# Frequency attention with real circulant matrices kept on chip, two rows a step

## The chip, the cores and the metric

The kernel runs on one core of a Trainium2 chip. The metric is the time on the device in microseconds (us), the median of several executions. All data are 32-bit floats.

## The reference

Two layers work on `x` of shape (8, 128, 128, 128): 8 images, 128 channels, 128 x 128 pixels. The change lies in the first layer, after a group norm:

```python
xf = jnp.fft.fft2(x)                                   # per image and channel
qf = xf.reshape(b, HEADS, hd, h * w)                   # 8 heads of 16 channels
qn = _l2norm_lastdim(qf)
attn_f = jnp.einsum('bhcn,bhdn->bhcd', qn, qn) * temp_f[None]
attn_f = jax.lax.complex(softmax(attn_f.real, axis=-1), softmax(attn_f.imag, axis=-1))
out_cplx = jnp.einsum('bhcd,bhdn->bhcn', attn_f, qf)
out_f = jnp.abs(jnp.fft.ifft2(out_cplx)).reshape(b, c, h, w)
...                                                    # gate in frequency: out_f_l
fsa = _conv(jnp.concatenate([out_f, out_f_l], axis=1), projf_w)
...                                                    # spatial attention: out_s, out_s_l
ssa = _conv(jnp.concatenate([out_s, out_s_l], axis=1), projs_w)
return fsa + ssa                                       # the layer adds x
```

The second layer is a selective scan over the pixels. It follows another group norm and is not touched.

## The kernel before

The kernel is one program of five stages, written with a tile framework that gives each engine a list of instructions and adds the waits.

Stage A normalises the images into `XN` (and a mirrored copy `XR`), and makes the 1x1 convolutions for the spatial attention (`PQKVX`). There POOL copies pieces of `x` into planes (L318) while DVE scales `x` (L334). Stage B makes the frequency attention matrix of each image, `aF`, and the gated frequency output `OFL`. Stage C makes the spatial attention, and writes its values `VS` and the local part `LS`. Stage D, which the change rewrites, makes the frequency output `out_f` and the projection of all four parts. Stage E is the second layer; there every instruction is recorded under L157, the line of the helper `InOrder`, which issues the instructions of an engine in the written order.

Stage D takes the images one after the other. For each it has two phases.

In the first phase the attention works along the image's rows instead of on a transform. `aF[:, b]` holds 128 cosine sums and 128 sine sums of the attention. `mix(i)` takes four rows of `XN` (`d_xn`, RB = 4) and the four rows' constants (`ker`, three 128 x 128 matrices a row, loaded from memory anew for every image). For each row one matmul with `aF` gives 256 columns (`d_a`, L641), and one DVE copy for two rows brings them to SBUF (`pq`, L642). `back(i)` runs one step later. For each row two accumulating matmuls of 256 columns with `ker` give the real and the imaginary part (`d_b`, L653 and L654). ACT squares both (`sq`, L655), POOL adds the squares (L656), and ACT writes the root into `of` (L657), which holds the whole image.

In the second phase the image is projected in 32 places of 512 pixels. Each place loads `OFL` (`d_of`) and `x` (`d_x`), every fourth place a band of `VS` and `LS` (`d_vs`, `d_ls`, 1 MB each). Four matmuls (L689 to L692) accumulate in `d_p`. DVE adds `d_x` and writes `x1` (L695), takes the statistics of the next group norm (L696), and POOL's queue stores it into `X1` (L697; the profile calls the tile `x` and the store `X`).

All loads of stage D stand in SP's queue. Pools with 3 buffers (`d_k`, `d_w`) or 2 (`d_v`) let loads run ahead; `of` has a single buffer. A load that waits for its buffer holds up the loads behind it in the queue.

Of the kernel before, what the change touches and what calls it, by code (L numbers as in the profile page):

```python
# [39 lines left out]
_CONSTS = [  # L40
    "ident", "group4", "mask", "neg", "c16", "s16", "first", "tc", "cm", "sm", "sneg", "a1", "a2", "blocks", "small",
    "cmp", "smp",
]


def _constants():
    i = np.arange(128)
    ang = 2 * np.pi * np.outer(i, i) / 128
    cos, sin = np.cos(ang), np.sin(ang)
    block = (i[:, None] // HD == i[None, :] // HD).astype(np.float64)  # L50
    u = np.arange(1, 64)

    tc = np.concatenate([cos[:, 64:65], sin[:, u], cos[:, u], cos[:, 0:1]], 1)
    a1 = np.concatenate([cos[64:65], 2 * sin[u], 2 * cos[u], cos[0:1]], 0) / HW
    a2 = np.concatenate([cos[64:65], 2 * cos[u], -2 * sin[u], cos[0:1]], 0) / HW
    made = {
        "ident": np.eye(128),
        "group4": (i[:, None] // 4 == i[None, :] // 4) / 4.0,
        "mask": block,
        "neg": (block - 1) * 1e30,  # L60

        "c16": block * np.cos(2 * np.pi * np.outer(i, i) / HD) / HD,
        "s16": block * np.sin(2 * np.pi * np.outer(i, i) / HD) / HD,
        "first": block * (i[None, :] % HD == 0) / HD,

        "cmp": cos.reshape(128, 32, 4).transpose(0, 2, 1).reshape(128, 128),
        "smp": sin.reshape(128, 32, 4).transpose(0, 2, 1).reshape(128, 128),
        "tc": tc, "cm": cos, "sm": sin, "sneg": -sin, "a1": a1, "a2": a2,
    }


    kind, quarter = i // 16 % 2, i // 32
    made["blocks"] = (kind[:, None] == i[None, :] // 64) & (quarter[:, None] == i[None, :] // 16 % 4)
    small = np.zeros((128, 128))
    small[:, 0:32] = i[:, None] % 32 == i[None, :32]
    small[:, 32:64] = kind[:, None] == i[None, :32] // 16
    small[:, 64:80] = i[:, None] % 16 == i[None, :16]
    small[:, 80:82] = kind[:, None] == i[None, :2]
    made["small"] = small

    ker = np.exp(2j * np.pi * np.outer(np.arange(HW), i) / HW).mean(1)
    ker = ker[(128 * (i[None, None, :] - i[:, None, None]) + i[None, :, None]) % HW]
    ker = np.stack([-ker.imag, ker.real, ker.imag], 2)
    return (
        np.concatenate([made[n] for n in _CONSTS], 1).astype(np.float32),
        ker.astype(np.float32),
    )
# [6 lines left out]
def _layout(a):  # L94
# [3 lines left out]
    o["consts"], o["ker"] = _constants()  # L98
# [4 lines left out]
    ws = [a[p + n + "1_w"].reshape(C, C) for n in "qkv"] + [f[:, :C], f[:, C:], s[:, rows], s[:, C:]]  # L103
# [64 lines left out]
def tile_kernel(ctx: ExitStack, tc: tile.TileContext, I: dict, out: bass.AP):  # L168
# [26 lines left out]
    def const(name, n=1):  # L195
        i = _CONSTS.index(name)
        return cst[:, i * 128 : (i + n) * 128]

    eye = const("ident")
# [14 lines left out]
    aF = keep.tile([128, B, 256], F32, name="aF")  # L214
# [144 lines left out]
    with tc.tile_pool(name="b_x", bufs=1) as xp_, tc.tile_pool(name="b_g", bufs=1) as gp_, tc.tile_pool(  # L359
        name="b_w", bufs=3  # L360
    ) as wk, tc.tile_pool(name="b_s", bufs=2) as sp_, tc.tile_pool(name="b_ps", bufs=8, space=PSUM) as psum:
        xh = xp_.tile([128, C, W], F32, name="xh")
# [16 lines left out]
        for b in range(B):  # L379
# [54 lines left out]
            nc.tensor.matmul(fp[:, :256], lhsT=att, rhs=const("c16", 2), start=True, stop=True)  # L434
            nc.vector.tensor_copy(aF[:, b, 0:128], fp[:, 0:128])
            nc.vector.tensor_tensor(aF[:, b, 128:256], fp[:, 128:256], const("first"), ALU.add)
# [172 lines left out]

    with tc.tile_pool(name="d_o", bufs=1) as op_, tc.tile_pool(name="d_v", bufs=2) as vp_, tc.tile_pool(  # L610
        name="d_k", bufs=3
# [3 lines left out]
        RB = 4  # L615
        of = op_.tile([128, W, RB, H // RB], F32, name="of")
        for b in range(B):
            ab = sp_.tile([128, 128], F32, name="ab")
            nc.vector.tensor_tensor(
# [5 lines left out]
            nc.tensor.matmul(mp[:, :128], lhsT=ab, rhs=weight("ps1"), start=True, stop=True)  # L625
            mT = sp_.tile([128, 128], F32, name="mT")
            nc.vector.tensor_copy(mT, mp[:, :128])
            st = sp_.tile([128, 32, 6], F32, name="st")
            live = {}

            def mix(i):

                xn = kp.tile([128, RB, W], F32, name="d_xn")
                nc.sync.dma_start(xn.rearrange("p h w -> p (h w)"), XN[b, :, i * RB * W : (i + 1) * RB * W])
                ker = kp.tile([128, RB, 3, 128], F32, name="ker")
                nc.sync.dma_start(ker, I["ker"][:, i * RB : (i + 1) * RB])
                pq = wk.tile([128, RB, 256], F32, name="pq")
                for j in range(0, RB, 2):
                    ps = psum.tile([128, 2, 256], F32, name="d_a", tag="ps")
                    for r in range(2):  # L640
                        nc.tensor.matmul(ps[:, r, :], lhsT=xn[:, j + r, :], rhs=aF[:, b, :], start=True, stop=True)  # L641
                    nc.vector.tensor_copy(pq[:, j : j + 2, :], ps)  # L642
                live[i] = (pq, ker)

            def back(i):

                pq, ker = live.pop(i)
                sq = wk.tile([128, RB, 2, 128], F32, name="sq")
                for j in range(0, RB, 2):
                    ps = psum.tile([128, 2, 256], F32, name="d_b", tag="ps")  # L650
                    for r in range(2):
                        kr = ker[:, j + r].rearrange("p t m -> p (t m)")
                        nc.tensor.matmul(ps[:, r, :], lhsT=pq[:, j + r, 0:128], rhs=kr[:, 128:384], start=True, stop=False)  # L653
                        nc.tensor.matmul(ps[:, r, :], lhsT=pq[:, j + r, 128:256], rhs=kr[:, 0:256], start=False, stop=True)  # L654
                    nc.scalar.activation(sq[:, j : j + 2], ps.rearrange("p r (t m) -> p r t m", t=2), AF.Square)  # L655
                nc.gpsimd.tensor_tensor(sq[:, :, 0, :], sq[:, :, 0, :], sq[:, :, 1, :], ALU.add)  # L656
                nc.scalar.activation(  # L657
                    of[:, :, :, i].rearrange("p m e -> p e m"), sq[:, :, 0, :], AF.Sqrt
                )

            n = H // RB
            for i in range(n + 1):
                if i < n:
                    mix(i)
                if i:
                    back(i - 1)
            off = of.rearrange("p m e j -> p (m e j)")
            band = {}
            for i in range(HW // 512):
                px = slice(i * 512, (i + 1) * 512)  # L670
                ld = {}
                for name, frm in (("of", OFL), ("x", I["x"])):
                    ld[name] = wk.tile([128, 512], F32, name=f"d_{name}")
                    nc.sync.dma_start(ld[name], frm[b, :, px])
                if i % 4 == 0:
                    for name, frm in (("vs", VS), ("ls", LS)):
                        band[name] = vp_.tile([128, 16, 4, 32], F32, name=f"d_{name}")

                        of_ = frm[b].rearrange("g (s k n) m -> s k g n m", s=4, k=2)[i // 8]
                        for kd in range(2):  # L680
                            nc.sync.dma_start(
                                band[name][64 * kd : 64 * kd + 64].rearrange("p n i j -> p n (i j)"),
                                of_[kd][:, :, i // 4 % 2 * 128 : i // 4 % 2 * 128 + 128],
                            )
                for name in ("vs", "ls"):
                    ld[name] = band[name][:, :, i % 4, :]
                ps = psum.tile([128, 512], F32, name="d_p", tag="ps")
                by4 = ps.rearrange("p (n j) -> p n j", j=32)
                nc.tensor.matmul(ps, lhsT=weight("pf2"), rhs=ld["of"], start=True, stop=False)  # L689
                nc.tensor.matmul(by4, lhsT=mT, rhs=ld["vs"], start=False, stop=False)  # L690
                nc.tensor.matmul(by4, lhsT=weight("ps2"), rhs=ld["ls"], start=False, stop=False)
                nc.tensor.matmul(ps, lhsT=weight("pf1"), rhs=off[:, px], start=False, stop=True)  # L692
                x1 = wk.tile([128, 512], F32, name="x1")
                nat = [t.rearrange("p (y j e) -> p y e j", y=4, e=4) for t in (x1, ld["x"])]
                nc.vector.tensor_tensor(nat[0], ps.rearrange("p (y e j) -> p y e j", y=4, e=4), nat[1], ALU.add)  # L695
                nc.vector.bn_stats(st[:, i, :], x1)  # L696
                nc.gpsimd.dma_start(X1[b, :, px], x1)  # L697
# [396 lines left out]
```

## Time and profile before

| | us |
|---|---|
| median of 3 executions | 21334.16 (21333.18 to 21354.21) |
| profiled execution, its own time | 21360.55 |
| profiled execution, span | 21358.5 |

| engine | busy us | share of the span | instructions |
|---|---|---|---|
| PE (matmul) | 18573.9 | 87% | 360816 |
| DVE | 13875.6 | 65% | 14884 |
| ACT | 11748.4 | 55% | 25436 |
| POOL | 11924.1 | 56% | 7116 |

The granted TensorE clock is 0.945 of full speed in the mean. Stage A ends at about 1850 us, B at 4300, C at 6520, D at 9120, and E takes the rest. A group of instructions in the profile is named by its line, its engine, its operation and its tiles (output<-inputs); after the bar stand the busy time, the mean time of one in ns, and the time that the engine was idle just before them with what ended it. Where a matmul works on 32-bit floats, the profile has two records for one matmul of the program.

### The profile page before, as it was taken

The page shows a single profiled execution, that of the slowest core. Times are in us where ns is not written, and L with a number is a line of the kernel's source. Part 1 is how long each engine was busy: PE and PEld are TensorE (multiplying, and loading weights), DVE is VectorE, ACT ScalarE, POOL GpSimd, SP SyncE. Part 2 cuts the span into 40 slices and gives each one's busy share as a digit, 9 for nine tenths or more (in the row PEclk, how much of TensorE's full clock was granted, in tenths as well). Part 3 has the DMA queues.
Part 4 walks back from the last instruction along what each step waited for, and adds up shares of the span by engine and source line. Part 5 has one row for each costly group of instructions (what it writes and reads, how often), then busy time and mean ns, then how long its engine had stood idle before and what let it go on. Part 6 is the DMA issues. An engine that isn't in the chain of part 4 may idle for free.

```text
span 21358.5 us, 802425 instructions
## 1 busy us (share of the span) xinstructions
PE 18573.9 (87%) x360816; PEld 10741.9 (50%) x360816; DVE 13875.6 (65%) x14884; ACT 11748.4 (55%) x25436; POOL 11924.1 (56%) x7116
## 2 busy tenths in 40 slices
PE   5647889889998898988989999898998989989898
PEld 3335667644546565644444444444444444444444
DVE  3332111133332333379999999999999999999999
ACT  2222222222222221267777777777777777777777
POOL 2221000000001111178889889898888888989888
PEclk8878999988889999999999999999999999999999
DMA  9996333255557888854444444444444444444443
GB/s 275 277 278 171 82 82 77 67 201 195 194 193 218 235 228 237 226 109 97 94 102 96 99 97 95 103 96 100 95 95 101 96 100 96 98 101 96 103 96 84
DMA packets 2989828, 2929.13 MB, mean 137 GB/s; under 512 B 1480494, under 2 KB 2275630, under 8 KB 2981667
## 3 DMA queue, kind: packets, MB, share of 16 engines
q1 hardware_dynamic: 2274818, 2537.53, 46.9%
q10 hardware_dynamic: 672672, 206.02, 4.5%
q0 software_dynamic: 38912, 134.24, 2.0%
q8 instruction: 2842, 46.56, 0.9%
q14 instruction: 584, 4.78, 0.1%
HBM read 1975.21 MB, written 902.04 MB: 135 GB/s over the span
## 4 chain that ended last, share of the span: by engine, by line
PE 53%; DVE 19%; ACT 12%; DMA 8%; issue 6%; SPq 2%; POOL 1%; DVEq 0%; ACTq 0%; POOLq 0%
DVE hs L157 14%; PE hb L157 9%; PE c_mm L529 6%; PE y L157 4%; PE e_xc L157 4%; ACT dA L157 4%; ACT L157 4%; DVE bd L157 3%; DMA d_ls<-LS 2%; PE e_z L157 2%; PE x_q L471 2%; PE d_a L641 2%; PE f_gram L426 2%; PE c_gram L574 2%; PE a_mm L308 2%
## 5 line engine op out<-in xcount | busy, mean ns | idle before, releaser
L157 POOL TENSOR_TENSOR hc<-hs,crep 128x1024 f32<-128x1024 f32 x4096 | 9648.7, 2374 | 1308.3 <-DVE hs L157 808.1
L157 DVE TENSOR_TENSOR_SCAN hs<-dA,state,hb 128x512 f32<-128x512 f32 x7936 | 9584.5, 1263 | 854.3 <-PE hb L157 788.4
L157 PEld LDWEIGHTS hb<-bd,duT 64*32 64x32 f32 x262144 | 3749.3, 106 | 3751.0 <-issue 2769.6
L157 PE MATMUL hb<-bd,duT 64*32 64x128 f32 x262144 | 4925.4, 275 | 727.8 <-issue 507.7
L157 ACT ACTIVATE dA<-dlrep,A 128x512 f32<-128x512 f32 x8192 | 5443.4, 713 | 6.9 <-ACT state L157 0.8
L157 PE MATMUL e_xc<-u,wf 128*128 128x512 f32 x4096 | 2255.5, 644 | 412.1 <-ACT u L157 365.4
L656 POOL TENSOR_TENSOR sq<-sq 128x512 f32<-128x512 f32 x256 | 324.5, 1268 | 3269.8 <-ACT sq L655 3269.8
L157 PE MATMUL y<-hc,gath 128*32 128x512 f32 x16384 | 2090.2, 611 | 12.9 <-issue 11.4
L157 ACT COPY state<-hs 128x2 f32<-128x2 f32 x4096 | 776.6, 190 | 1903.4 <-DVE hs L157 1885.5
L529 PE MATMUL c_mm<-src,taps 32*32 32x512 f32 x32768 | 1522.0, 657 | 168.9 <-ACT junk L540 74.7
L157 ACT ACT_TABLE_LOAD x1023 | 1312.5, 1283 | 346.1 <-PE e_dt L157 287.6
L493 POOL DMA_DIRECT2D OFL<-ya x128 | 113.6, 887 | 2448.2 <-ACT ya L490 2448.2
L529 PEld LDWEIGHTS c_mm<-src,taps 32*32 32x32 f32 x32768 | 636.0, 107 | 992.2 <-issue 399.7
L157 ACT ACTIVATE bd<-same,bt 128x64 f32<-128x64 f32 x4096 | 1054.6, 339 | 29.6 <-PE hb L157 29.3
L157 PEld LDWEIGHTS e_xc<-u,wf 128*128 128x128 f32 x4096 | 650.7, 193 | 835.3 <-ACT u L157 425.2
L157 DVE TENSOR_TENSOR bd<-same,e_bt 128x512 f32<-128x512 f32 x1536 | 1023.3, 666 | 0.0
L460 DVE TENSOR_TENSOR pr<-x_x,G 128x512 f32<-128x512 f32 x256 | 264.9, 1035 | 1127.5 <-PE x_x L456 1127.5
L232 ACT ACTIVATE gn_sd<-gn_gv,eps 128x1 f32<-128x1 f32 x16 | 4.2, 261 | 1741.6 <-PE gn_gv L230 1741.6
L642 DVE COPY pq<-d_a 128x512 f32<-128x512 f32 x512 | 354.1, 692 | 930.8 <-PE d_a L641 930.8
L308 PE MATMUL a_mm<-xt,wp 128*128 128x256 f32 x3072 | 746.6, 397 | 91.4 <-ACT pv L315 56.1
L554 ACT COPY vst<-c_mm 128x512 f32<-128x512 f32 x256 | 149.8, 585 | 1222.4 <-PE c_mm L529 908.2
L695 DVE TENSOR_TENSOR x<-d_p,d_x 128x512 f32<-128x512 f32 x256 | 276.0, 1078 | 822.7 <-PE d_p L692 718.4
(198 smaller groups left out, 22965.9 us busy)
## 6 DMA issues: line engine op xcount, KB each, us to landing
dlrep<-dld SPq DMA_DIRECT2D x2048, 256.0 KB
crep<-cd SPq DMA_DIRECT2D x2048, 128.0 KB
ker<-in_ker SPq DMA_DIRECT2D x256, 768.0 KB
dld<-dl SPq DMA_DIRECT2D x256, 512.0 KB
src<-Pq SPq DMA_DIRECT2D x128, 544.5 KB
src<-Pv SPq DMA_DIRECT2D x128, 544.5 KB
src<-Pk SPq DMA_DIRECT2D x128, 544.5 KB
src<-Px SPq DMA_DIRECT2D x128, 544.5 KB
```

The source lines that it names most:

```text
L157: made = method(*args, **kwargs)
L308: nc.tensor.matmul(ps[:, y : y + 2], lhsT=weight("qkv"[n]), rhs=now, start=True, stop=True)
L426: nc.tensor.matmul(gram[:, :128], lhsT=xh[:, :, (W - 64 * d - v) % W], rhs=xr[:, :, v], start=(d == 1 and v == 0), stop=(d == 0 and v == 63),)
L460: nc.vector.tensor_tensor(pr.rearrange("p c (t s) -> p c t s", t=2), xs.rearrange("p c (t s) -> p c t s", t=2), gate, ALU.mult)
L471: nc.tensor.matmul(qp[:, c], lhsT=pr[:, 2 * i + c, :], rhs=const("cmp", 2).rearrange("p (t w) -> p t w", t=2), start=True, stop=True,)
L529: nc.tensor.matmul(banks[r][32 * s : 32 * s + 32].rearrange("p f (i j) -> p f i j", j=32), lhsT=taps[rs, gq, cv, o, :], rhs=grid[rs, :, y0 ...
L554: nc.scalar.copy(o, ps)
L574: nc.tensor.matmul(gram[32 * j : 32 * j + 32, :], lhsT=qm[:, :, :, f, n].rearrange("p a g -> p (a g)"), rhs=kk[:, :, f, n], start=(n < 4), ...
L641: nc.tensor.matmul(ps[:, r, :], lhsT=xn[:, j + r, :], rhs=aF[:, b, :], start=True, stop=True)
L642: nc.vector.tensor_copy(pq[:, j : j + 2, :], ps)
L656: nc.gpsimd.tensor_tensor(sq[:, :, 0, :], sq[:, :, 0, :], sq[:, :, 1, :], ALU.add)
L695: nc.vector.tensor_tensor(nat[0], ps.rearrange("p (y e j) -> p y e j", y=4, e=4), nat[1], ALU.add)
```

## The change

Stage D is written anew, and its constants with it.

1. The complex constant of a row is split into a phase and a real circulant matrix. `ker` is one real 128 x 128 matrix a row, 8.4 MB for all rows, and stays in SBUF for the whole stage. ACT's queue loads it once in eight pieces.
2. The phase goes onto the mixed rows: the result of the mix is scaled by a cosine and by a sine (`d_cs`, from two columns of `first`), and four additions or subtractions combine them into `pq`. Of the 16 real and imaginary rows of a head only 9 cosine and 8 sine rows differ (`NJ` = 9); `aF` has 2 x 72 columns instead of 256. Row j and row 16-j come from the same sums, so `pq` has a part for `t` (real, imaginary) and for `up` (the rows below 8, the mirrored ones).
3. A step takes two rows instead of four. For a pair u: two `d_a` matmuls of 144 columns; two scalings, both on DVE for even u, one on ACT for odd u; three additions on DVE, one on POOL; two steps later four `d_b` matmuls of 128 columns, ACT's square, POOL's addition; another step later ACT's root. The pools of these tiles have 2 buffers.
4. The order of PE, DVE, ACT and POOL in stage D is that of the text (`InOrder`), so their instructions are recorded under the helper's line. Loads are issued ahead in the text: two pieces of `d_xn`, three places, two bands.
5. The projection adds into `d_x` itself and stores from it; `x1` is gone. `pf1` comes first among its four matmuls.
6. The constants that only stages B to D use come in a second tile `bcst`, loaded at the start of stage B; `cst` is smaller. The rows of the projection's weights are ordered to suit.

```diff
-        RB = 4
+        pe, dve, act, gps = (InOrder(tc, e) for e in (nc.tensor, nc.vector, nc.scalar, nc.gpsimd))
+        RB, NR_ = 4, NH * NJ
         of = op_.tile([128, W, RB, H // RB], F32, name="of")
+        ker = op_.tile([128, H, 128], F32, name="ker")
+        for i in range(8):
+            nc.scalar.dma_start(ker[:, 16 * i : 16 * i + 16], I["ker"][:, 16 * i : 16 * i + 16])
+        cosw, sinw = const("first")[:, 126:127], const("first")[:, 127:128]
...
+        def mix(b, u):
+            xn = live["xn", b, u // 2]
+            ps = psum.tile([128, 512], F32, name="d_a", tag="ps")
+            for r in range(2):
+                pe.matmul(
+                    ps[:, 2 * NR_ * r : 2 * NR_ * (r + 1)], lhsT=xn[:, u % 2 * 2 + r, :], rhs=aF[:, b, :], start=True, stop=True
+                )
+            cs = kp.tile([128, 2, 2, 2 * NR_], F32, name="d_cs")
+            frm = ps[:, : 4 * NR_].rearrange("p (r s) -> p r s", r=2)
+            if u % 2:
+                act.activation(cs[:, :, 0], frm, AF.Copy, scale=cosw)
+            else:
+                dve.tensor_scalar(cs[:, :, 0], frm, cosw, None, ALU.mult)
+            dve.tensor_scalar(cs[:, :, 1], frm, sinw, None, ALU.mult)
...
+            pq = live["pq", b, u] = kp.tile([128, 2, 2, 2, 64], F32, name="pq")
+            for eng, t, up, op in (
+                (dve, 0, 0, ALU.subtract), (gps, 0, 1, ALU.add), (dve, 1, 0, ALU.add), (dve, 1, 1, ALU.subtract)
+            ):
+                js = slice(up, up + 8)
+                eng.tensor_tensor(
+                    pq[:, :, t, up].rearrange("p r (h j) -> p r h j", j=8), a[t][:, :, :, js], b_[1 - t][:, :, :, js], op
+                )
+
+        def back(b, u):
+            pq = live.pop(("pq", b, u))
+            ps = psum.tile([128, 2, 2, 128], F32, name="d_b", tag="ps")
+            for r in range(2):
+                for t in range(2):
+                    pe.matmul(
+                        ps[:, r, t], lhsT=pq[:, r, t].rearrange("p k s -> p (k s)"), rhs=ker[:, 2 * u + r, :],
+                        start=True, stop=True,
+                    )
+            sq = kp.tile([128, 2, 2, 128], F32, name="sq")
+            act.activation(sq, ps, AF.Square)
+            gps.tensor_tensor(sq[:, :, 0], sq[:, :, 0], sq[:, :, 1], ALU.add)
+            live["sq", b, u] = sq
+
+        def root(b, u):
+            e = u % 2 * 2
+            act.activation(of[:, :, e : e + 2, u // 2].rearrange("p m e -> p e m"), live.pop(("sq", b, u))[:, :, 0], AF.Sqrt)
+
+        def project(b, i, st, mT):
...
+            x1 = live.pop(("x", b, i))
+            nat = x1.rearrange("p (y j e) -> p y e j", y=4, e=4)
+            dve.tensor_tensor(nat, ps.rearrange("p (y e j) -> p y e j", y=4, e=4), nat, ALU.add)
+            dve.bn_stats(st[:, i, :], x1)
+            gps.dma_start(X1[b, :, px], x1)
...
+            for u in range(NU_ + 3):
+                if u < NU_:
+                    mix(b, u)
+                    if u % 2 and u // 2 + 2 < H // RB:
+                        load_rows(b, u // 2 + 2)
+                if 0 <= u - 2 < NU_:
+                    back(b, u - 2)
+                if 0 <= u - 3:
+                    root(b, u - 3)
...
+            for i in range(NP):
+                project(b, i, st, mT)
+                if i + 3 < NP:
+                    load_place(b, i + 3)
+                if i % 4 == 3 and i // 4 + 2 < NP // 4:
+                    load_band(b, i // 4 + 2)
```

## The prediction

> **What bounds the kernel now.** I began with the slices of the page: the span is 21358.5 us and four stages follow each other. The edit sits in the fourth, where `d_` tiles are at work, so I asked for the busy time of each engine in stretches there (columns: stretch, its length, PE, PEld, DVE, ACT and POOL busy, granted clock, DMA share, GB/s).
>
> ```profile
> 6520.00:6690.00 170.00, 169.11 (x771) 148.43 (x772) 45.25 (x68) 72.53 (x96) 39.38 (x31) 0.98 0.63 203
> 6690.00:6850.00 160.00, 128.87 (x268) 55.45 (x267) 59.06 (x73) 1.80 (x3) 18.61 (x33) 0.90 1.03 253
> ```
>
> An image takes two phases, and they have different limits. In the first (mix and back) PE is busy all the time and DMA 63%. In the second (projection) PE has gaps and the DMA engines are full. The first `d_a` matmul starts at 6521.3 and the last projection add of the eighth image at 9119.7, so the stage is 2600 us, 325 us an image. The groups of instructions of this stage (busy us, mean ns of one, idle before it and who ended it):
>
> ```profile
> L654 PE MATMUL d_b<-ker,pq 128*128 128x256 f32 x2048 | 609.1, 379 | 0.0
> ...
> L642 DVE COPY pq<-d_a 128x512 f32<-128x512 f32 x512 | 354.1, 692 | 930.8 <-PE d_a L641 930.8
> L656 POOL TENSOR_TENSOR sq<-sq 128x512 f32<-128x512 f32 x256 | 324.5, 1268 | 3269.8 <-ACT sq L655 3269.8
> L691 PE MATMUL d_p<-d_ls,wp 128*128 128x512 f32 x512 | 305.2, 681 | 209.3 <-DMA d_ls<-LS 209.3
> L655 ACT ACTIVATE sq<-d_b 128x512 f32<-128x512 f32 x512 | 305.1, 597 | 421.1 <-PE d_b L654 421.1
> ...
> L657 ACT ACTIVATE of<-sq 128x512 f32<-128x512 f32 x256 | 278.7, 1089 | 367.8 <-POOL sq L656 367.7
> ```
>
> PE never waits in `d_b`; DVE, ACT and POOL wait for PE. The timeline gives PE 5.18 us per step of four rows (the four `d_a` matmuls start at 6530.82, 6536.00, 6541.18). That is 12 matmuls of 256 columns, 0.43 us each, 1.68 ns a column. So the first phase is 32 x 5.18 = 166 us plus 3 us to start, **169 us**, and the projection is the remaining **156 us**, in which `d_ls` is what PE waits for.
>
> The change puts much small work on DVE and POOL. Whether these two run side by side is told by stage A, where POOL copies while DVE works (count: shortest/median/longest ns):
>
> ```profile
> L275 DVE TENSOR_TENSOR m<-m x8: 151/153/154, 36.4 to 1594.9; 128x1 f32<-128x1 f32 x8
> L277 DVE TENSOR_TENSOR m<-m x8: 367/368/370, 37.2 to 1595.7; 128x1 f32<-128x1 f32 x8
> L318 POOL COPY px<-xt x1024: 392/412/1072, 36.5 to 1744.8; 128x128 f32<-128x128 f32 x171
> ```
>
> L275 and L277 are the same tiny operation. The first runs ahead of POOL's first copy, the second during the copies, and takes 0.215 us longer all eight times. The copies themselves stretch to 1072 ns. Two SBUF-reading instructions of DVE and POOL hold each other up.
>
> [...] they show 0.2 us, not a whole 0.4 us copy. [...] Here a 128-element tensor_tensor takes 277 to 292 ns (L619, L246), more than double its 133 ns of elements (692 ns at 512 elements against 291 at 128 is 1.04 ns an element). [...] The trace gives (2374 - 1268) / 512 = 2.16 ns an element and 0.16 us fixed. [...] The `X` store takes 6.0 us at the median.
>
> **The change, first phase, per pair of rows u (64 an image).**
> - PE: two mixes of 144 columns and four backs of 128, instead of 1536 columns: 800 x 1.68 ns = **1.35 us** (before 2.59). Its weight loads double relative to columns; the eight 128-column `x_y` passes with new weights each take 0.89 us (3001.37 to 3002.26), the full rate, so this holds.
> - DVE: the copy (692) goes. Scalings of 288 elements out of PSUM come, 1.5 on average: 480 ns at 256 (L313) and 744 at 512 (L544) give 0.51 us; successive L313 instructions start 0.08 us before the last one ends, so 0.43 net. Three additions of 128 elements: 0.28, net 0.21. Sum 0.65 + 0.63 = **1.28 us**.
> - POOL: one addition of 128 (0.44) and one of 256 (0.72), **1.16 us**.
> - ACT: square 0.60, half a scaling 0.21, root 256 wide by half of 1089 plus the fixed part, 0.64: **1.45 us**.
>
> No engine alone reaches 2.59. But the order is fixed, and POOL's addition into `pq` waits for the same two scalings as DVE's three; the `sq` addition stands right behind it. Both then read SBUF while DVE does its additions. The second DVE addition waits for the first POOL one to have read (0.28 us of elements, 0.25 net) and the third for the second (0.55, 0.50 net). With 0.1 us for the handovers: 1.28 + 0.75 + 0.1 = **2.15 us** a pair, DVE bound. The two ends for this unseen overlap: no contention, 1.45 to 1.8 (ACT or DVE); whole instructions exclusive, 2.6 to 2.9. I take the middle, as L277 lost half a copy. The loops through two buffers don't set the pace: PE is done with back(u-2) some 1.4 us after DVE finished that pair (0.5 for a mix ahead of it, 0.9 for itself), and DVE writes that `pq` again only after 2.15 + 0.43 us. Phase: 64 x 2.15 + 5 us to fill and drain three steps = **143 us, minus 26**.
>
> **Projection.** Its DMA must be counted. An image moves 5 x 8.4 = 42 MB there. Before, 3.6 MB of it came early (three places, one band), and 3 MB of `ker` and `d_xn` for the next image went along: 41.4 MB in 156 us. Now two bands and three places come early and no `ker`: 36.8 MB, 139 us at 265 GB/s. Against it: the sum is now written into the tile `d_x`, so the load of place i+3 waits for the store of place i to land (6 us), and SP's queue holds the next `d_of` and the band behind that wait. The loop load, add, store is about 4 + 1.1 + 0.3 + 6 us over three places, 3.8 us, below the 4.8 us per place that DMA gives, so it costs some of the early issue, not the pace. I take **minus 4** an image (from minus 17 to plus 8).
>
> **Waits added.** At the start of an image `d_xn` of step u=4 stands in SP's queue behind a band, three places and the landing of the last stores: 3.7 MB, 14 us, when it is wanted after 12: plus 3. In the first image the 8.4 MB of `ker` on ACT's queue and 5.7 MB on SP's queue share the engines ahead of it: 11 MB at 270 GB/s is 41 us, wanted after 10: plus 30, once. ACT's instructions behind the `ker` issues start late by the same cause. `bcst`, 0.8 MB ahead of `xh` at the start of stage B, plus 3 at 275 GB/s; `cst`, smaller by the same 0.8 MB ahead of the first `x`, minus 2 to 3, as `wp` still shares the engines there. Smaller `aF` work in B: 8 pairs of instructions, nothing, hidden behind nothing but below 1 us. Stages A, C and E keep their order.
>
> Sum: 8 x (-26 - 4) + 7 x 3 + 30 + 1 = **-188 us** on the profiled 21360.55. That execution lies 26 us (0.12%) above the median of 21334.16, and I put the difference on the median: **21146 us**, 0.9% faster. Under 0.2% (43 us) a difference can't be told from none.
>
> **Rivals.**
> 1. DVE and POOL hardly meet (POOL's addition falls in the scalings, which read PSUM): 1.6 us a pair, 107 us a phase, 8 x (-62 - 6) + 52 = -490, 20840 us. For it: L334's 0.80 us scalings in stage A grow only to 0.83 beside the copies. Against: POOL's pair starts exactly with DVE's additions. Chance 0.18.
> 2. Exclusive instructions: DVE and POOL alternate, 0.84 + 1.16 us under one lock plus 0.65 of scalings and gaps, 2.9 us; 64 x 2.9 + 5 = 191, plus 22 an image: 8 x 18 + 52 = +195, 21530 us, **slower**. It decides from 2.5 us a pair on (8 x (64 x 2.52 + 5 - 169 - 4) = -52). For it: [...]copies of 1072 ns. Against: L277's 0.215 us. Slower POOL additions on runs of eight elements lead here too. Chance 0.27.
> 3. The store in place of `x1` empties the DMA engines: 5.6 us a place, +23 an image, which eats the first phase's gain: 8 x (-26 + 23) + 52 = +28, 21360 us, no change. Against: DMA backlog of 6 to 11 us per band before. Chance 0.08.
>
> The forecast's own case has 0.47 and runs from 20980 to 21290. The range takes in most of rivals 1 and 2: 20780 to 21490. Slower: 0.24 of rival 2 and 0.02 of rival 3, 0.26. Same: 0.03 and 0.05 of them, 0.08. Faster: the own case, rival 1 and a rest of rival 3, 0.66.
>
> **What will show it.** `d_b` matmuls of two neighbouring pairs 2.15 us apart; DVE's three additions unequal, one near 0.28, the others near 0.5 and 0.75 us, and POOL's stretched or not; PE idle ended by DVE `pq`. Projection 150 us with POOL stores ahead of SP's waits. If the three additions are all 0.28, rival 1 holds; if POOL's are stretched too and a pair takes 2.6 or more, rival 2. The forecast is wrong if PE still never waits in `d_b`.

## The result and the profile after

The changed kernel takes 21392.23 us (median of 12 executions, 21352.92 to 21415.84). The kernel before takes 21334.6 us beside it (12 executions). The ratio is **1.0026, with a 95% interval of 1.0017 to 1.0034**: slower by 0.26%, about 57 us. The forecast was 0.9% faster.

The profiled execution of the changed kernel is 26 us under its median, and that of the kernel before was 26 us over its own. The two spans therefore differ by 6 us only (21364.5 against 21358.5), and what is compared below is the stage, not the span.

From the timeline of PE each image's two phases can be measured: the mix phase from its first `d_a` to its last `d_b` matmul, the projection from its first to its last `d_p` matmul. Summed over eight images (us):

| | before | after | difference |
|---|---|---|---|
| mix phases | 1341.3 | 1251.9 | -89 |
| projections | 1222.4 | 1331.5 | +109 |
| gaps between phases | 34.4 | 53.8 | +19 |
| stage D | 2598.1 | 2637.2 | **+39** |

The mix phase fell from 168 to 154 us an image, and the projection rose from 153 to 166. The remaining 18 us of the 57 have no place in the traces: there, what comes ahead of stage D is 24 us shorter after the change and what follows it 9 us. A difference of this size need not come from the change: in the trace of e5 below, whose text ahead of stage D is that of the kernel before, the stage begins 25 us earlier too (6496.0 against 6521.5).

First the projection. The busy times in most of the changed kernel's second projection (columns: stretch, its length, PE, PEld, DVE, ACT and POOL busy, granted clock, DMA share, GB/s):

```profile
7011.00:7168.00 157.00, 116.37 (x238) 49.50 (x236) 52.45 (x60) 0.00 (x0) 16.20 (x30) 0.87 0.92 231
```

The same projection of the kernel before:

```profile
7025.00:7167.00 142.00, 115.55 (x236) 48.20 (x234) 51.37 (x58) 0.00 (x0) 15.67 (x29) 0.89 1.06 259
```

The engines do the same work in both. The DMA share fell from 1.06 to 0.92 and the rate from 259 to 231 GB/s: the DMA engines, which set the pace before, now run empty at times. What SP's queue waits for longest in that projection shows why (queue, line of the waiting load, what it waits for: us in total, times, longest). First the kernel before, then the changed one:

```profile
SPq L674 <- DVE x L695: 72.2, 20, 8.2
SPq L662 <- DMA X<-d_x: 95.5, 19, 8.1
```

L674 and L662 are the load of a place. Before, SP stood until DVE had added out of `d_x`, and the DMA engines were full all the same. Now it stands for 95.5 of 157 us until a store out of `d_x` has landed. In the timeline of SP's queue one sees who stands behind it:

```profile
7061.68 1.30 SPq L654 DMA_DIRECT2D d_vs<-VS  x2
7070.68 0.33 SPq L662 DMA_DIRECT2D d_x<-in_x  x1
7071.11 1.29 SPq L654 DMA_DIRECT2D d_ls<-LS  x2
7072.49 2.32 SPq L662 DMA_DIRECT2D d_of<-OFL  x1
```

From 7063.0 to 7070.7 nothing is issued. The band `d_ls` and the next `d_of`, 1.3 MB whose buffers have nothing to do with the store, go out only after the `d_x` load. By then the DMA engines have little left to do (columns as above):

```profile
7070.00:7072.00 2.00, 2.00 (x6) 0.92 (x5) 1.68 (x2) 0.00 (x0) 0.54 (x1) 1.00 0.27 35
```

Now the mix phase. A stretch of it in the second image, columns as above:

```profile
6910.00:6930.00 20.00, 15.81 (x108) 13.01 (x106) 19.06 (x41) 12.24 (x22) 11.65 (x19) 1.00 0.24 65
```

DVE is busy for 19.06 of 20 us, PE for 15.81, and DMA is at 24%: DVE is the bound. The same is seen in the groups of instructions of stage D (busy us, mean ns of one, idle before it and who ended it):

```profile
L167 DVE TENSOR_TENSOR pq<-d_cs 128x128 f32<-128x128 f32 x1536 | 745.2, 538 | 61.2 <-PE d_b L167 9.0 <-DVE d_cs L167 1.4
L167 PE MATMUL d_b<-ker,pq 128*128 128x128 f32 x4096 | 708.0, 299 | 213.4 <-DVE pq L167 175.5 <-POOL pq L167 7.0
...
L167 PE MATMUL d_a<-aF,d_xn 128*128 128x144 f32 x2048 | 353.1, 299 | 115.1 <-DMA d_xn<-XN 101.8 <-DMA ker<-in_ker 13.3
...
L167 PE MATMUL d_p<-d_of,wp 128*128 128x512 f32 x512 | 317.2, 706 | 318.5 <-DMA d_of<-OFL 318.5
```

PE now waits for DVE's `pq`; in the projection, its waits for `d_of` stand for the empty DMA engines. DVE's additions take 538 ns on the mean, and are of three kinds: of the 1536, 550 take up to 0.30 us, 504 some 0.55 and 477 some 0.81. The view of the tile `pq` (shortest/median/longest ns):

```profile
L167 DVE TENSOR_TENSOR pq<-d_cs x1536: 276/552/818, 6499.8 to 8964.9; 128x128 f32<-128x128 f32 x192
L167 POOL TENSOR_TENSOR pq<-d_cs x512: 459/552/577, 6499.9 to 8964.2; 128x128 f32<-128x128 f32 x171
```

The timeline shows two pairs of rows of the second image (start, length; x3 is three instructions in a row):

```profile
6929.93 1.49 DVE L167 TENSOR_TENSOR pq<-d_cs 128x128 f32<-128x128 f32 x3
6929.97 0.57 POOL L167 TENSOR_TENSOR pq<-d_cs 128x128 f32<-128x128 f32 x1 [0.72 <-ACT of L167]
6930.51 0.77 POOL L167 TENSOR_TENSOR sq<-sq 128x256 f32<-128x256 f32 x1
...
6931.34 0.93 DVE L167 TENSOR_SCALAR d_cs<-d_a,cst 128x288 f32<-128x288 f32 x2
...
6934.40 0.29 DVE L167 TENSOR_TENSOR pq<-d_cs 128x128 f32<-128x128 f32 x1
```

Two pairs take 6934.40 - 6929.93 = 4.47 us, 2.235 a pair. POOL's two additions run from 6929.97 to 6931.28 and DVE's three until 6931.42, 0.14 us after POOL's second. The same three additions take 0.28, 0.55 and 0.82 us.

### The profile page after: what moved, and what is told of

Read it like the earlier page. It is cut to its first block, busy times and chain, and to the rows that moved or that the text cites. A ratio compares the mean times of both kernels' runs of the same rounds, so it can differ in the third digit from the quotient of the medians.

```text
span 21364.5 us, 807127 instructions
## 1 busy us (share of the span) xinstructions
PE 18151.7 (85%) x360816; PEld 10369.2 (49%) x360816; DVE 14594.2 (68%) x16676; ACT 11869.3 (56%) x25948; POOL 12262.2 (57%) x7884
## 5 line engine op out<-in xcount | busy, mean ns | idle before, releaser
L167 POOL TENSOR_TENSOR pq<-d_cs 128x128 f32<-128x128 f32 x512 | 285.2, 557 | 2801.2 <-DMA d_xn<-XN 2192.8
L167 DVE TENSOR_TENSOR d_x<-d_p,d_x 128x512 f32<-128x512 f32 x256 | 276.6, 1081 | 911.6 <-PE d_p L167 820.5
L167 PE MATMUL d_b<-ker,pq 128*128 128x128 f32 x4096 | 708.0, 299 | 213.4 <-DVE pq L167 175.5
L167 POOL DMA_DIRECT2D X<-d_x x256 | 138.5, 541 | 1214.1 <-DVE d_x L167 1184.1
```

Source lines behind the costliest of these rows:

```text
L167: made = method(*args, **kwargs)
```

## The experiments

Each ratio is against the kernel before on the same chip, with its 95% interval. The changed kernel wasn't run again beside them; "against the changed kernel" is the difference of the two ratios times 21335 us, good to some 40 us. The mean phases of an image and the sum of the gaps between phases, measured as above (us):

| kernel | mix, image 1 | mix, others | projection | gaps, sum | stage D | ratio to before |
|---|---|---|---|---|---|---|
| before | 168 | 168 | 152.8 | 34.4 | 2598 | 1 |
| after | 174.7 | 153.9 | 166.4 | 53.8 | 2637 | 1.0026 |
| e5_before_inplace | 168.4 | 167.9 | 167.0 | 34.8 | 2714 | 1.0057 [1.0042, 1.0072] |
| e1_own_x1 | 174.2 | 150.3 | 153.0 | 71.5 | 2522 | 0.9962 [0.9947, 0.9977] |
| e8_x_other_queue | 173.9 | 146.8 | 155.9 | 98.9 | 2548 | 0.9978 [0.9971, 0.9985] |
| e3_late_loads | 168.7 | 144.6 | 166.3 | 56.0 | 2567 | 0.9989 [0.9983, 0.9996] |
| e2_no_pool | 159.0 | 138.4 | 165.9 | 52.0 | 2507 | 0.9952 [0.9935, 0.9968] |
| e10_pool_pq_only | 162.2 | 142.0 | 165.1 | 52.9 | 2530 | 0.9972 [0.9962, 0.9982] |
| e9_pool_sq_only | 142.5 | 120.5 | 165.9 | 55.1 | 2368 | 0.9879 [0.9863, 0.9896] |
| e4_psum_inputs | 140.1 | 119.1 | 165.3 | 56.0 | 2352 | 0.9875 [0.9860, 0.9889] |
| e7_three_undone | 153.8 | 128.1 | 152.1 | 69.3 | 2337 | 0.9859 [0.9843, 0.9876] |
| e6_best_guess | 135.0 | 108.4 | 152.3 | 71.7 | 2184 | 0.9815 [0.9800, 0.9830] |
| e11_together | 136.6 | 110.1 | 151.1 | 71.4 | 2188 | 0.9792 [0.9776, 0.9808] |

### The store in place

The theory is that the sum written into `d_x` costs the projection its 14 us, by the wait of the loads for the landing of the store. The rival is that something else of the rewrite does (the order of the four matmuls, the missing `ker` loads, more loads issued early). One experiment does this part of the change alone, in the kernel before:

```diff
-                x1 = wk.tile([128, 512], F32, name="x1")
+                x1 = ld["x"]
```

> The kernel before with one part of the change alone: the projection adds into d_x and stores from it, no x1. Theory: the projection phase grows from 152.5 us by the same 14 us or a little more, 110 us in all, about 21445 us. Rival (order of the loads): no change, 21335 us.

Measured: 21422.85 us, +0.57% or 122 us, all in the projection, which goes from 152.8 to 167.0 us while the mix phase stays at 168. This one line costs more than the whole change does.

The other undoes it in the changed kernel. Here `x1` has two buffers; in the kernel before it has three:

```diff
-            x1 = live.pop(("x", b, i))
-            nat = x1.rearrange("p (y j e) -> p y e j", y=4, e=4)
-            dve.tensor_tensor(nat, ps.rearrange("p (y e j) -> p y e j", y=4, e=4), nat, ALU.add)
+            x1 = wk.tile([128, 512], F32, name="x1", bufs=2)
+            nat = [t.rearrange("p (y j e) -> p y e j", y=4, e=4) for t in (x1, live.pop(("x", b, i)))]
+            dve.tensor_tensor(nat[0], ps.rearrange("p (y e j) -> p y e j", y=4, e=4), nat[1], ALU.add)
```

> The changed kernel with one part undone: the projection adds into a tile x1 of its own (two buffers) and stores from it. Theory (the store out of d_x holds back SP's loads, 747.6 us of waits for the X store): SP's waits for that store go, the projection phase falls from 166.5 us to about 151 us (DMA share from 0.92 back to 1.0 or more), 8 x 15 = 120 us less, about 21270 us. Rival (the projection is slower because of the written order of places and bands in SP's queue): projection stays near 166 us, the time near 21390 us.

Measured: 21222.44 us, 137 us less than the changed kernel, and a projection of 153.0 us. Its stretch in the second projection (columns as above):

```profile
6974.00:7116.00 142.00, 112.47 (x238) 48.25 (x237) 52.29 (x60) 0.00 (x0) 16.11 (x30) 0.93 1.02 255
```

The DMA engines are full again. The rival falls: on balance nothing else of the rewrite changes the projection (153.0 against 152.8 us before).

Does the landing itself cost the time, with three tiles, or that SP stands in it with other loads behind? The third experiment leaves the sum in `d_x` and moves only the loads of `d_x` to another queue:

```diff
-                nc.sync.dma_start(t, frm[b, :, i * 512 : (i + 1) * 512])
+                q = nc.scalar if name == "x" and i >= 3 else nc.sync
+                q.dma_start(t, frm[b, :, i * 512 : (i + 1) * 512])
```

> The changed kernel, with the loads of d_x for places 3 and later issued by ACT, which has no work in the projection, instead of SP; the sum is still written into d_x and stored from there. Theory 1 (the queue): what costs the 14 us an image is that SP, waiting for the store of place i, can't issue the d_of load and the bands behind it. Then these flow again, d_x itself has three tiles and a loop of 3.8 us a place, and the projection falls from 166 us to 153 to 157, 70 to 105 us less than the changed kernel (which is 57 above the one before): 15 to 50 us under the one before. Theory 2 (the tiles): three tiles held through the landing of the store are too few, whoever issues. Then the projection stays near 166 us and the time near the changed kernel's, 40 to 70 us above the one before.

Measured: 21176.04 us beside 21220.9 before, 102 us less than the changed kernel. The projection takes 155.9 us. So 10.5 of the 13.4 us that a tile of its own wins back are had by moving the `d_x` loads to another queue. The other 3 us may be the late `d_x` itself, which was not tried further. Nor was a second queue tried together with a tile of its own, so what it would win where no load waits for a store isn't known. The gaps between phases grow from 53.8 to 98.9 us, so that the stage gains 89 us where that of e1 gains 115. Waits for `X` stores all but vanish from SP's queue over the whole stage, first the changed kernel, then e8:

```profile
SPq L662 <- DMA X<-d_x: 747.6, 162, 8.9
```

```profile
SPq L663 <- DMA X<-d_x: 23.4, 7, 4.7
```

### The loads ahead of the mix phase

In the changed kernel PE stalls at the fifth step of an image for `d_xn`, which stands behind bands and places in SP's queue. In e3 those are issued at pairs 17 to 41:

```diff
-            for i in range(2):
-                load_band(b, i)
-            for i in range(3):
-                load_place(b, i)
...
+                if u in (17, 25):
+                    load_band(b, u // 25)
+                if u in (33, 37, 41):
+                    load_place(b, (u - 33) // 4)
```

> The changed kernel with the first two bands and three places of an image loaded in the middle of the first phase (pairs 17 to 41) instead of ahead of it. Theory (d_xn of pair 4 stands behind 3.7 MB in SP's queue): the stall of 10 us at the head of images 2 to 8 and of 28 us in the first goes, 60 to 95 us less, about 21310 us, projection unchanged. Rival (the stall is the bandwidth that the last stores and, in the first image, ker take, not the queue's order): less than 30 us gained.

Measured: 21269.25 us, 79 us less than the changed kernel; the mix phase falls from 153.9 to 144.6 us and the projection is as it was. The stall of the second image in PE's timeline, in the changed kernel:

```profile
6862.74 1.30 PE L167 MATMUL d_a<-aF,d_xn 128*128 128x144 f32 x4 [9.88 <-DMA d_xn<-XN]
```

and with late loads:

```profile
6833.04 0.73 PE L167 MATMUL d_a<-aF,d_xn 128*128 128x144 f32 x4 [1.28 <-DMA d_xn<-XN]
```

The stall goes from 9.88 to 1.28 us. For the first image the theory held in small part only: its 28 us were expected to go too, and PE still waits 13.3 and 10.2 us for `d_xn` there (mix phase 168.7 us instead of 174.7). That fits the rival, that `ker`'s loads share the DMA engines at that time, but was not tested by itself. Moving these loads costs the projection nothing, here or in e7 and e11 below, where it is not held back by the stores.

### DVE and POOL

Both additions of POOL were given to DVE:

```diff
-                (dve, 0, 0, ALU.subtract), (gps, 0, 1, ALU.add), (dve, 1, 0, ALU.add), (dve, 1, 1, ALU.subtract)
+                (dve, 0, 0, ALU.subtract), (dve, 0, 1, ALU.add), (dve, 1, 0, ALU.add), (dve, 1, 1, ALU.subtract)
...
-            gps.tensor_tensor(sq[:, :, 0], sq[:, :, 0], sq[:, :, 1], ALU.add)
+            dve.tensor_tensor(sq[:, :, 0], sq[:, :, 0], sq[:, :, 1], ALU.add)
```

> The changed kernel with POOL's two additions of the first phase given to DVE; POOL only issues stores. Theory (DVE and POOL hold each other up on SBUF reads): DVE's 128-element additions fall from 0.55 us at the median to 0.28 us, a pair takes 0.65 + 4 x 0.21 + 0.35 + 0.1 = 1.95 us instead of 2.24, 64 x 8 x 0.29 = 150 us less, about 21240 us, though DVE has more to do. Rival (the additions are slow in themselves, by their runs of eight elements): they stay near 0.5 us, a pair takes 0.65 + 4 x 0.45 + 0.6 = 3.0 us, 390 us more, about 21780 us.

Measured: 21198.72 us, 158 us less than the changed kernel. The timeline of DVE for one pair:

```profile
6939.83 0.90 DVE L167 TENSOR_TENSOR pq<-d_cs 128x128 f32<-128x128 f32 x4
...
6940.65 0.42 DVE L167 TENSOR_TENSOR sq<-sq 128x256 f32<-128x256 f32 x1
```

Four additions take 0.90 us where three took 1.49. DVE does two instructions more and is done sooner: a pair takes 1.98 us.

To size the two hold-ups, each of POOL's additions was left alone in turn. First only the one into `sq` (the first line of the diff above without the second):

> The changed kernel with only POOL's addition into pq given to DVE; POOL keeps the one into sq. Theory 1 (each of POOL's two additions holds one of DVE's up for the time of its elements, 0.25 and 0.5 us): the sq addition starts when ACT's square is ready, which in the kernel without POOL additions falls in the middle of DVE's four; so one addition still takes about 0.8 us, four take 0.9 + 0.5 = 1.4 us instead of 1.5 for three, and a pair comes to about 2.1 us: 8 to 10 us less an image, 60 to 80 us less than the changed kernel, near 20 under the one before. Theory 2 (the sq addition only did harm because it stood behind the pq addition): freed from it, it falls beside the scalings, which read PSUM; then a pair takes 1.6 to 1.7 us and 35 us an image go, 220 under the kernel before.

Measured: 20986.85 us beside 21240.93 before, **314 us less than the changed kernel**. My theory failed here, and the rival held. The timeline of DVE, POOL and ACT over two pairs:

```profile
6802.58 0.91 DVE L167 TENSOR_TENSOR pq<-d_cs 128x128 f32<-128x128 f32 x4
6802.71 0.60 ACT L167 ACTIVATE sq<-d_b 128x512 f32<-128x512 f32 x1
...
6803.41 0.51 DVE L167 TENSOR_SCALAR d_cs<-d_a,cst 128x288 f32<-128x288 f32 x1
6803.45 0.73 POOL L167 TENSOR_TENSOR sq<-sq 128x256 f32<-128x256 f32 x1 [0.72 <-ACT sq L167]
...
6805.89 0.90 DVE L167 TENSOR_TENSOR pq<-d_cs 128x128 f32<-128x128 f32 x4
```

ACT's square ends at 6803.31, when DVE is about done with its four additions. POOL's addition then runs beside the scaling, which reads PSUM and takes its usual 0.51 us. The view of the tile `pq` has DVE's additions short at the median; a few tens still meet POOL's:

```profile
L167 DVE TENSOR_TENSOR pq<-d_cs x2048: 275/279/839, 6428.7 to 8623.8; 128x128 f32<-128x128 f32 x187
```

A pair takes (6805.89 - 6802.58) / 2 = 1.655 us. In the changed kernel the `sq` addition was driven into DVE's additions by the order on POOL: it stood right behind the `pq` addition, which starts with DVE's.

Then only the one into `pq` (the second line without the first):

> The changed kernel with only POOL's addition into sq given to DVE; POOL keeps the one into pq. Theory 1 (as for the other half): one of DVE's three additions into pq takes about 0.55 us, the others 0.28, so three take 0.66 + 0.06 + 0.28 = 1.0 us and the sq addition 0.34 to 0.42 more; with 0.72 for the scalings a pair takes 2.05 us, 12 us less an image, 95 us less than the changed kernel, 40 under the one before. The two halves together are then worth about as much as both at once (158). Theory 2 (almost all of the loss is the first hold-up, since it delays what stands behind it): no gain, within 30 us of the changed kernel.

Measured: 21181.24 us, 115 us less than the changed kernel, and a pair of 2.045 us. The view of the tile `pq`:

```profile
L167 DVE TENSOR_TENSOR pq<-d_cs x1536: 276/293/558, 6413.3 to 8772.7; 128x128 f32<-128x128 f32 x192
L167 POOL TENSOR_TENSOR pq<-d_cs x512: 460/549/578, 6413.4 to 8772.1; 128x128 f32<-128x128 f32 x171
```

One addition of three is held up, to at most 558 ns, and none reaches 818. So 0.28 us of hold-up belong to POOL's `pq` addition and 0.54 to its `sq` addition, as the first theory says of this half. What that theory got wrong is that the `sq` addition must meet DVE's.

Is it reading SBUF twice that is held up, or any DVE instruction? In e4 the additions read one operand from PSUM, scaled in the same instruction; the scalings shrink to 144 elements, and POOL keeps `sq`:

```diff
-                eng.tensor_tensor(
-                    pq[:, :, t, up].rearrange("p r (h j) -> p r h j", j=8), a[t][:, :, :, js], b_[1 - t][:, :, :, js], op
-                )
+                dve.scalar_tensor_tensor(
+                    pq[:, t, up].rearrange("p (h j) r -> p h (j r)", j=8), a[:, :, js], sinw if t else cosw,
+                    b_[1 - t][:, :, js], ALU.mult, op,
+                )
```

> The changed kernel with the four additions into pq all on DVE as scalar_tensor_tensor, which scales one operand straight from PSUM and adds or subtracts the other from SBUF; so the scalings shrink from 288 to 144 elements, no DVE addition has two SBUF inputs, and POOL keeps only the addition into sq (still 0.77 us, still beside DVE's additions). Theory 1 (what holds DVE up is two-input SBUF reading on both engines at once): the additions are all alike, 0.25 to 0.33 us each, 1.0 to 1.3 in all, plus 1.5 scalings of 0.3: 1.5 to 1.75 us a pair, 32 to 41 us an image, 260 to 330 us less than the changed kernel, so 200 to 270 under the one before. Theory 2 (any DVE instruction beside POOL's is held up): the additions beside the sq addition stay at 0.5 us and more, a pair stays at 2.0 us or above, and the time is within 130 us of the changed kernel's. A third outcome would be PE: the weights of d_b are now read with a stride of two elements; if that slows the loads, d_b's matmuls lie further apart than 0.17 us and PE no longer waits for pq.

Measured: 20965.16 us, 322 us less than the changed kernel. The timeline of DVE and POOL, and the view of the tile `pq`:

```profile
6803.73 0.73 POOL L167 TENSOR_TENSOR sq<-sq 128x256 f32<-128x256 f32 x1 [1.05 <-ACT sq L167]
6804.02 1.13 DVE L167 SCALAR_TENSOR_TENSOR pq<-d_a,cst,d_cs 128x128 f32<-128x128 f32 x4
```

```profile
L167 DVE SCALAR_TENSOR_TENSOR pq<-d_a,cst,d_cs x2048: 339/343/354, 6413.2 to 8594.1; 128x128 f32<-128x128 f32 x187
```

Here POOL's addition (6803.73 to 6804.46) does lie beside DVE's, and yet all 2048 of them take 339 to 354 ns, though about half overlap one of POOL's by more than 0.1 us. DVE's additions with one operand in PSUM are not held up here. The weights of `d_b`, read with a stride of two elements, load in 197 ns instead of 192: no third outcome.

### Together

e7 joins e1, e2 and e3:

> The changed kernel with the three remedies tried one at a time put together: the sum in a tile x1 of its own, POOL's two additions given to DVE, the first bands and places of an image issued at pairs 17 to 41. Against the changed kernel they gave -137, -158 and -78 us. If the three costs lie in different stretches (projection, pair pace, start of an image) they add up: -373, which is 316 us under the kernel before. If they hide each other, say because a shorter mix phase leaves the loads that come early less time and the projection pays for it, at least 80 us of it is missing.

Measured: 20928.66 us beside 21220.9 before, 356 us less than the changed kernel where the three alone sum to 373 (136.5 + 157.9 + 78.9). The costs add up to within the 40 us. e6 joins e1, e3 and e4:

> The scalar_tensor_tensor form together with the tile x1 of its own and the late loads. If theory 1 of that form holds, -260 to -330 for it, -137 and -78 for the others: 475 to 545 us less than the changed kernel, 420 to 490 under the one before. If it does not hold, 160 to 290 us under the one before. If the shorter mix phase only moves the waiting to the DMA engines, it ends up near the other combination, 300 to 330 under.

Measured: 20834.61 us, 395 us under the kernel before, short of the 420 expected at least. In the stage it is 453 us under the changed kernel, where e1, e3 and e4 alone are 115, 70 and 285 under it: 17 us missing there. By the ratios 88 us are missing (538 - 450), not much more than the some 70 us to which the ratios in that sum are good. The last kernel joins e1, e3 and e9:

> The changed kernel with the addition of POOL into pq given to DVE (a pair then takes 1.65 us), the sum in a tile x1 of its own (projection 152 us) and the late loads (no stall for d_xn at the start of an image). If the three lie in different stretches: mix phase 64 x 1.65 + 2 = 108 us, projection 152 us, first image some 27 us more; against the kernel before, 8 x (168 + 153 - 108 - 152) - 27 = 460 us in the stage. The kernel with the additions read from PSUM has these phases too and gave 386 us, so 380 to 460 under the kernel before. If the two forms of the additions differed in more than when POOL's one addition falls, the phases would differ by over 3 us from 108 and 152.

Measured: 20801.96 us beside 21251.26 before: **0.9792, 444 us faster than the kernel before** and 499 us than the changed one. Its phases are 110.1 and 151.1 us.

## Why the prediction was wrong

The forecast had stage D 189 us shorter; it became 39 us longer in the trace, 228 us apart. Step by step:

- **The projection, the step that failed: 141 us.** Minus 4 an image was taken, +13.6 came (109 / 8). The prediction saw the wait for the landing and the queue behind it. It then put the loop of load, add, store and landing, 3.8 us a place, against the 4.8 us of DMA, and concluded that it costs early issue, not the pace. That comparison leaves out what stands behind the wait. For `d_x` alone it nearly holds, as e8 shows (155.9 us against 153.0 in e1). But SP stood in the wait with `d_ls` and `d_of` behind it, the DMA engines ran empty meanwhile (share 0.92), and a place came to 166.4 / 32 = 5.2 us. In substance this is rival 3, priced at 5.6 us a place, +23 an image and 21360 us, and given a chance of 0.08. The "DMA backlog of 6 to 11 us per band before" cited against it belongs to the kernel before, where loads are issued early, and that is what the wait takes away.
- **The pair of rows: nearly right.** 2.15 us was predicted and 2.235 came, with the unequal additions predicted (0.28, 0.5, 0.75 us against 276, 552 and 818 ns). The two hold-ups sum to 0.82 us instead of 0.75. Over 64 pairs and eight images that is 64 x 0.085 x 8 = 44 us. That DVE's second and third additions wait for POOL's was the author's estimate, from L277's 0.215 us. The wait was somewhat longer than it took: the third addition ended 0.14 us after POOL's 0.77 us one, and over all pairs of the changed kernel the second and the third each end 0.15 us after POOL's at the median. Whether POOL's additions wait for DVE's in the same way, the runs don't decide. They grew only from 459 to 552 ns and from 722 to 771. In the first pair shown POOL's first starts 0.04 us after DVE's first, which takes 0.28, and the prediction's 0.16 us of fixed time for POOL (from its additions of 2374 and 1268 ns in the kernel before) may pass meanwhile. By an estimate from these figures 0.08 us of waiting would show, against the 0.09 it grew. Rival 2, at 2.9 us a pair, fell on its size: it added whole instructions, 0.84 + 1.16 = 2.0 us, where the same five take 1.49 us, so part of each passes while the other engine works.
- **The stall at the start of an image: under-sized.** Plus 3 us was taken and 10.4 came on the mean of seven images, 52 us more in all. When `d_xn` would come was right: 12 + 3 us was forecast, and it is there 15 to 17 us after the image's first `d_a`. When it is wanted was wrong: PE stands after some 6 us, not 12 (in the second image from 6852.86, and the first `d_a` began at 6846.92), so the first four pairs' mixes go by at 1.5 us a pair, faster than DVE's pace of 2.235. e3 takes nearly all of the stall away. That the stores have a part in it isn't shown: the mix phases of e1 and e8 are 3.6 and 7.1 us shorter than the changed kernel's, but the gaps ahead of them are longer by 2.5 and 6.4 us, so most of that wait has only moved.
- **The first image: right.** 30 us were predicted for `d_xn` behind `ker` and the loads ahead; PE waited 28.00 us there, and the phase is 31 us longer than one without a stall.
- **Rival 1, no contention at 1.6 us a pair,** did not hold for this order of instructions, but e9 shows that it was one word away: with POOL's `pq` addition on DVE a pair takes 1.655 us.
- The prices of single instructions held: a scaling on DVE 504 ns (0.51 us taken), the root 648 (0.64), POOL's additions at their shortest 459 and 722 (0.44 and 0.72).
- **Filling, draining and the phase before: smaller terms.** 5 us an image were taken for filling and draining three steps. Some 0.5 us of that are in the mix phase and 2.4 in the longer gap after it, as PE starts the projection only after ACT's last root (a wait of 2.28 us): 17 us less in all. The first phase before was put at 169 us and measures 167.7, which takes 11 us from the gain. With the pair (44), the stall (52) and the first image (1) this makes 44 + 52 + 1 - 17 + 11 = 91 us, against the 87 that the projection leaves of the 228; 3 us of the difference are the forecast's rounding of 142.6 to 143.

So the mechanism of the mix phase was right and the pace of a pair nearly so; that no mix phase took the forecast's 143 us is due to the stall above all. The gain of 89 us there was more than eaten by one change of a buffer that the title of the change does not even mention.

## What to carry to other kernels

Before a result is written into the tile that was loaded, ask which queue will wait for the store to land and what stands behind that load: one line cost 122 us in the kernel before. Price a wait in a queue by all the loads behind it, not by the loop of the tile it protects: a place took 5.2 us here, where the loop came to 3.8. When POOL is to relieve DVE, look at what DVE reads at that moment: here POOL's two additions beside DVE's two-operand SBUF additions cost 158 us more than DVE doing them itself (e2), and in e4, where DVE's additions read one operand from PSUM, POOL's held none of them up (339 to 354 ns).

## What the runs showed of the hardware

- In the changed kernel and in e10 a DVE addition with two SBUF operands took 0.28 us longer beside a POOL addition of 128 elements, and in the changed kernel 0.54 us longer beside one of 256; there it ended 0.15 us after POOL's at the median in both cases. POOL's own took 552 and 771 ns at the median, 459 and 722 at the shortest. In e4 an addition with an operand in PSUM took its 339 to 354 ns beside POOL's too, and POOL's of 256 its 0.72 to 0.74 us.
- In stage A of the kernel before, the 422 copies of POOL that met only L313 of DVE, which reads PSUM, took 394 to 447 ns. The 37 that met only L334, which reads SBUF, took 417 to 892 ns, 875 at the median.
- In e2 four DVE additions of 286 ns each took 0.90 us in a row, 0.2 us from start to start. This overlap of 0.08 us is over a quarter of such an addition.
- The landing of an `X` store had a median of 6.0 us in the kernel before, 5.5 in the changed one and 5.7 in e1: the store did not become slower, only waited for.
